# A state-space convolution and a 4-bit feed-forward layer in one kernel: kernels of the first 16 heads made in groups of six and ten

## The chip, the core and the metric

The kernel runs on one core of one Trainium2 chip. The metric is the device time of one execution in microseconds (us). The core has a matrix engine (PE, with PEld for its weight loads), a vector engine (DVE), a scalar engine (ACT), GpSimd (POOL) and a sync engine (SP) whose queue issues most DMAs. Each engine works through its own queue in order and waits for others by semaphores.

## The reference

Input `x` is [32, 64, 1024] (batch, head, time). A diagonal state-space layer makes one causal convolution kernel of length 1024 for each of 64 heads and applies it under a length mask. A gated feed-forward layer follows, with 4-bit weights, and its result is added to `x`:

```python
K = 2.0 * einsum('hn,hnl->hl', Cs, exp(dtA[:, :, None] * arange(1024))).real
y = irfft(rfft(u * mask, 2048) * rfft(K, 2048))[..., :1024] + u * mask * D
y = y * mask
Wg, Wu, Wd = dequant(gate), dequant(up), dequant(down)
out = x + (silu(y2 @ Wg) * (y2 @ Wu)) @ Wd      # rows are (batch, head), 1024 columns
```

## The kernel before, in words

**Kernels of the heads.** A convolution kernel of 1024 taps is a 32 x 32 product of two factors over the 128 complex state parts. For a group of heads, `phase_tables` (L182 to L210) makes eight DVE steps (L192 to L204) that leave reduced phases in `r1` and `r2`, then four ACT steps: sine twice (L207) and square twice (L209). `decay_tables` (L165) makes the decay factors `xd`, one small exponential per head on ACT. `kernel_factors` (L213 to L224) turns both into `e1` and `e2` by five DVE steps. `make_kernel` (L421) multiplies them on PE in f32 (one tap row for `D`, L425, then two passes a head, L427), rounds the result to an f16 high part on ACT (L430) and a low part on DVE (L431), and writes both to `kpad` in DRAM by two DMAs on ACT's queue (L433). `toeplitz` (L512) then reads each head back on SP's queue as a 512 KB Toeplitz tile (L525). SP is in order: while one load waits for `kpad`, everything behind it on SP waits.

**Convolution.** `conv_head` does 24 f16 matmuls per head (L548). After each pair of heads DVE masks the result (`y`, L560), ACT makes the high half `xh` (L563) and POOL the low half `xl` (L565; DVE for head 15). `conv_split` and `conv_load` split the input of four heads into `uh` (ACT) and `ul` (DVE), L495, L497, L507 and L510.

**The lead.** Before the first convolution come the parameters, `head_coefficients` for 32 heads (short DVE steps in three sections), the decay tables of heads 0 to 15, then tables, factors, kernel and loads of heads 0 to 3, the same for heads 4 to 7, and tables and factors of heads 8 to 15. `busy` (L889) issues f32 matmuls whose result nobody reads: 16 passes behind the first kernel, 8 behind the second. The low part of the input, `conv_split(k)`, stands behind the factors.

**Events.** The loop `for i, _ in enumerate(c.conv(0))` steps through the convolution of heads 0 to 15, eight steps a head, and starts other work at given steps: at step 7 `kernel_8` (kernel of heads 8 to 15, decay tables of heads 16 to 31, input split 2 and 3, tables and factors of heads 16 to 23), at 56 the scale ratios of the feed-forward weights (`scale_ratios`, L410 to L418), at 63 ten more `busy` calls, at 75 the kernel of heads 16 to 23, at 87 the input of heads 16 to 19. Weight unpacking (L578 to L599) and the group of heads 24 to 31 (`group_24`) step along at further places.

**Order.** The instructions are put in order on each queue before the kernel runs, by program order and dependencies with some moves to fill gaps. `with c.after(key)` ties the instructions of the block on an engine behind the instruction of that engine that `mark` stored under `key`.

**Behind the lead.** The feed-forward stages follow; the first one (`gu_one`, L664 and L665 on PE) runs interleaved with the convolution of heads 16 to 31.

Of the kernel before, what the change touches and what calls it, by code (L numbers as in the profile page):

```python
# [163 lines left out]

def decay_tables(nc, pool, co, cst, h0):  # L165
    xd = pool.tile([128, 8, 64], F32, name=f"xd{h0 // 8}", bufs=1, tag=f"xd{h0 // 8 % 4}")
    for h in range(8):
        nc.scalar.activation(xd[:, h, :], cst[:, 0:64], AF.Exp, scale=co["na"][:, h0 + h:h0 + h + 1])
    return xd

# [12 lines left out]
def phase_tables(nc, side, pool, co, cst, h0, nh):  # L183
# [19 lines left out]
    stt(r1, r1, off1, pl, ALU.subtract, ALU.subtract)  # L203
    stt(r2, r2, off2, pl[:, :, 32:], ALU.subtract, ALU.subtract)  # L204
    yield
    for r in (r1, r2):
        nc.scalar.activation(r, r, AF.Sin, scale=3.1415925)  # L207
    for r in (r1, r2):
        sq_op = nc.scalar.activation(r, r, AF.Square, scale=1.4142135623730951)  # L209
    return r1, r2, sq_op  # L210


def kernel_factors(nc, pool, co, xd, s1, s2, h0, nh):  # L213
    tt, stt = nc.vector.tensor_tensor, nc.vector.scalar_tensor_tensor
    per = lambda a: a[:, h0:h0 + nh].unsqueeze(2).to_broadcast([128, nh, 32])
    t = lambda name: pool.tile([128, 8, 32], F32, name=name, bufs=2)[:, :nh, :]
    e1, e2 = t("e1t"), t("e2t")
    stt(e2, s1[:, :, :32], 1.0, xd[:, :, :32], ALU.subtract, ALU.mult)
    stt(e1, s1[:, :, 32:], 1.0, per(co["ab"][:, 0]), ALU.subtract, ALU.mult)
    yield  # L220
    stt(s2, s2, 1.0, per(co["ab"][:, 1]), ALU.subtract, ALU.mult)
    tt(e1, e1, s2, ALU.add)
    last = tt(e1, e1, xd[:, :, 32:], ALU.mult)
    return e1, e2, last  # L224
# [34 lines left out]
class Core:  # L259
# [145 lines left out]
    def scale_ratios(self, s16, nt, g, name, last_factor):  # L405
# [3 lines left out]
        s, z = self.take([128, nt, g], F32), self.take([128, nt, g], F32)  # L409
        nc.scalar.copy(s, s16)  # L410
        for t0, t1, p0, p1, f in last_factor:
# [9 lines left out]
    def make_kernel(self, pool, h0, nh, place):  # L421
# [4 lines left out]
        for h in range(nh):  # L426
            nc.tensor.matmul(q[:, h, :], e1[:, h, :], e2[:, h, :], start=False, stop=(h == nh - 1),  # L427
                             skip_group_check=True)
        kb = pool.tile([32, 2, 8, 32], F16, name="kb", bufs=2)[:, :, :nh, :]
        self.mark("act", nc.scalar.activation(kb[:, 0], q, AF.Copy, scale=KSCALE))  # L430
        self.mark(("kb", h0), nc.vector.scalar_tensor_tensor(kb[:, 1], q, KSCALE, kb[:, 0], ALU.mult, ALU.subtract))  # L431
        for k in range(2):
# [9 lines left out]

    def tables(self, pool, h0, nh):
        held = h0 >= 24
        steps = phase_tables(self.nc, self.nc.vector, pool, self.co, self.cst, h0, nh)
        while True:
            try:
                with self.after("dve" if held else None), self.after("act" if held else None):
                    next(steps)
            except StopIteration as done:  # L450
                self.tab, sq_op = done.value[:2], done.value[2]
                break
            self.dve(800)
# [37 lines left out]

    def conv_split(self, k, after, last="e"):
        u, uh, ul = self.us[k]
        with self.after(("sq", after)):
            self.nc.scalar.copy(uh, u)  # L495
        with self.after((last, after)):
            self.nc.vector.tensor_tensor(ul, u, uh, ALU.subtract)  # L497
        self.us[k] = uh, ul

    def conv_load(self, h0):  # L500
        nc = self.nc
        u = self.cv.tile([128, 8, 4, B], F32, name="u", bufs=1)
        self.mark("sp", nc.sync.dma_start(u.rearrange("p c h b -> p (c h b)"), self.io["xF"][h0 // 4]))
        uh = self.cv.tile([128, 8, 4, B], F16, name="uh")
# [339 lines left out]
def tile_ssm_ffn(ctx, tc, io):  # L844
# [38 lines left out]
    c.taps(kg, 16)  # L883
    xd = [decay_tables(nc, kg, co, c.cst, h0) for h0 in (0, 8)]
    section(steps)
# [3 lines left out]
    def busy(h0, n):  # L889
        e1, e2 = (e.rearrange("p h n -> p (h n)") for e in c.fac[h0])  # L890
        for _ in range(n):
            nc.tensor.matmul(c.psum("wq", "b")[:, 0, :128], e1, e2, start=True, stop=True)

    for k, h0 in enumerate((0, 4)):
        every(c.tables(tables, h0, 4))
        every(c.factors(kg, h0, 4, xd[0][:, h0:h0 + 4]))
        c.make_kernel(kg, h0, 4, "b")
        for h in range(h0, h0 + 4):
            c.t0[h] = c.toeplitz(h)
        busy(h0, 8 - 4 * k)  # L900
        c.conv_split(k, h0)
    every(c.tables(kg, 8, 8))
    every(c.factors(kg, 8, 8, xd[1]))
    c.masks()
    tc.no_sync_barrier()

    def group_24():
        yield from c.tables(kg, 24, 8)
        yield from c.factors(kg, 24, 8, xd[3])
        while c.forced:  # L910
# [16 lines left out]

    def kernel_8():
        c.make_kernel(kg, 8, 8, "b")
        with c.after("act"):  # L930
            xd.extend(decay_tables(nc, kg, co, c.cst, h0) for h0 in (16, 24))
        for k in (2, 3):
            c.conv_split(k, 8, "kb")
        steps = c.tables(kg, 16, 8)
        next(steps)
        next(steps)
        with c.after(("kb", 8)):
            every(steps)
        every(c.factors(kg, 16, 8, xd[2]))

    def load_16():
        c.us[4] = c.conv_load(16)

    events = {7: kernel_8, 63: lambda: busy(4, 10), 56: ratios_gu, 87: load_16, 75: lambda: c.make_kernel(kg, 16, 8, "b")}
    for i, _ in enumerate(c.conv(0)):
        if i in events:
            with c.after("dve" if i == 56 else None):
                events[i]()
        if i in (32, 40, 48, 56, 64, 72, 104, 116, 124):
            next(unpack_it)  # L950
# [170 lines left out]
```

## Time and profile before

| quantity | value |
| --- | --- |
| time of three runs | 1069.36, 1070.72, 1071.31 us (median 1070.72) |
| profiled execution | 1069.87 us, of it span 1068.1 us |
| mean granted clock of PE | 0.996 |
| PE busy | 1023.9 us (96%) |
| DVE busy | 807.2 us (76%) |
| ACT busy | 775.7 us (73%) |
| POOL busy | 247.2 us (23%) |
| first matmul of the first convolution | 24.38 us from the span's start |
| last matmul of head 15 ends | 58.3 us |
| first feed-forward matmul (L664) | 62.00 us |

Times in the text are counted from the start of the span. A line of the timeline has the start, the length, engine, source line, operation, tiles out and in, shape and count; in brackets stands the idle time before it and what ended it. A line that merges several instructions (x24) has the length of all together. A line of the chain of waits has start, length, and what the chain ran through.

### The profile page before, as it was taken

What the parts mean: (1) busy time and instruction counts of PE and PEld (TensorE: products, weight loads), DVE (VectorE), ACT (ScalarE), POOL (GpSimd) and SP (SyncE); (2) the same over time, 40 slices, a digit from 0 to 9 for tenths busy, and PEclk for the clock granted to TensorE, in tenths of its full rate; (3) what the DMA queues carried; (4) which work ended last, traced back from release to release, by engine and by line L of the source; (5) the groups of instructions that cost most, each with busy time, mean ns of one, the idle gap of its engine ahead of it and who ended that gap; (6) DMA issues with size and microseconds to landing.
All of it is one profiled execution on the core that took longest, in us unless ns stands there. A gap on an engine that the chain in (4) does not pass through costs nothing.

```text
span 1068.1 us, 15388 instructions
## 1 busy us (share of the span) xinstructions
PE 1023.9 (96%) x5854; PEld 512.2 (48%) x5854; DVE 807.2 (76%) x938; ACT 775.7 (73%) x1036; POOL 247.2 (23%) x270
## 2 busy tenths in 40 slices
PE   3989999999899999999999999999999999999996
PEld 2867444444344445555565444444444444444442
DVE  8965788888987787886456767777787777777776
ACT  5767778787677778777777776666666667778775
POOL 0333233232332242223012112222211122102102
PEclk9999999999999999999999999999999999999999
DMA  6976311111111435448652001000000002424002
GB/s 196 331 248 205 108 70 40 40 60 40 36 54 50 140 91 164 147 135 280 214 168 99 30 30 50 20 20 18 13 21 21 20 21 62 146 79 154 34 1 79
DMA packets 52099, 99.76 MB, mean 93 GB/s; under 512 B 9524, under 2 KB 11444, under 8 KB 52024
## 3 DMA queue, kind: packets, MB, share of 16 engines
q1 hardware_dynamic: 38888, 70.09, 20.6%
q0 software_dynamic: 5280, 17.31, 4.3%
q10 hardware_dynamic: 7856, 11.37, 3.7%
q8 instruction: 46, 0.75, 0.3%
q14 instruction: 29, 0.24, 0.1%
HBM read 78.99 MB, written 19.76 MB: 92 GB/s over the span
## 4 chain that ended last, share of the span: by engine, by line
PE 78%; DVE 8%; issue 5%; ACT 5%; DMA 3%; POOL 1%; DVEq 0%; SPq 0%; ACTq 0%; POOLq 0%
PE chq L687 22%; PE chq L688 21%; PE chq L736 11%; PE chq L737 11%; PE cq L548 6%; PE chq L665 2%; PE chq L664 2%; ACT chq L640 1%; DVE chq L618 1%; DVE v L700 1%; DMA t<-kpad 1%; DVE chq L637 1%; ACT chq L620 1%; DMA xr<-xT 1%; POOL spill L310 1%
## 5 line engine op out<-in xcount | busy, mean ns | idle before, releaser
L687 PE MATMUL chq<-xh,w 128*128 128x512 f16 x1216 | 459.5, 379 | 7.7 <-DVE chq L618 3.3
L688 PE MATMUL chq<-xl,w 128*128 128x512 f16 x1216 | 457.6, 379 | 0.0
L618 DVE TENSOR_SCALAR chq<-chq,gur 128x1024 f32<-128x1024 f32 x261 | 333.3, 1290 | 93.7 <-PE chq L688 93.2
L620 ACT ACTIVATE chq<-chq,gur 128x1024 f32<-128x1024 f32 x285 | 304.4, 1085 | 86.6 <-PE chq L688 85.2
L640 ACT ACTIVATE chq<-chq,dnr 128x512 f32<-128x512 f32 x374 | 242.8, 661 | 74.1 <-PE chq L737 68.1
L736 PE MATMUL chq<-ihl,wd 128*128 128x512 f16 x672 | 253.1, 379 | 2.5 <-DVE wd L599 0.9
L737 PE MATMUL chq<-ihl,wd 128*128 128x512 f16 x672 | 252.6, 379 | 0.0
L637 DVE TENSOR_TENSOR chq<-chq,dnr 128x1024 f32<-128x1024 f32 x128 | 156.5, 1231 | 75.9 <-PE chq L737 75.2
L688 PEld LDWEIGHTS <-w 128*128 128x128 fp8e4 x1216 | 118.7, 98 | 156.2 <-issue 20.5
L687 PEld LDWEIGHTS <-w 128*128 128x128 fp8e4 x1216 | 118.8, 98 | 146.7 <-issue 1.2
L310 POOL TENSOR_TENSOR ihl<-v,ihl 128x512 f16<-128x512 f32 x42 | 48.3, 1149 | 363.5 <-ACT ihl L629 363.5
L737 PEld LDWEIGHTS <-wd 128*128 128x128 fp8e4 x672 | 65.6, 98 | 71.3 <-issue 6.7
L736 PEld LDWEIGHTS <-wd 128*128 128x128 fp8e4 x672 | 65.5, 98 | 68.4 <-DVE wd L599 2.0
L548 PEld LDWEIGHTS <-t 128*128 128x128 f16 x1152 | 80.8, 98 | 35.5 <-DMA t<-kpad 1.9
L548 PE MATMUL cq<-uh,t 128*128 128x256 f16 (+3 forms) x720 | 90.5, 226 | 1.7 <-DMA t<-kpad 1.7
L548 PE MATMUL cq<-ul,t 128*128 128x256 f16 (+3 forms) x360 | 71.5, 225 | 0.0
L565 POOL TENSOR_TENSOR xl<-y,xh 128x512 f16<-128x512 f32 x28 | 36.8, 1313 | 144.7 <-ACT xh L563 144.7
L629 ACT CAST ihl<-v 128x512 f16<-128x512 f32 x42 | 25.9, 617 | 58.8 <-DVE v L700 55.4
L700 DVE SCALAR_TENSOR_TENSOR v<-chq,gul,sg 128x1024 f32<-128x1024 f32 x38 | 48.7, 1280 | 17.2 <-PE chq L688 11.4
L310 POOL TENSOR_TENSOR spill<-v,spill 128x512 f16<-128x512 f32 x42 | 48.7, 1160 | 14.2 <-ACT spill L629 13.9
L640 ACT ACTIVATE chq<-chq,gur 128x512 f32<-128x512 f32 x66 | 43.2, 661 | 11.4 <-PE chq L665 10.2
L590 POOL TENSOR_TENSOR w<-w,z 128x256 int32<-128x256 int32 x42 | 31.6, 772 | 81.2 <-DVE w L584 77.5
(256 smaller groups left out, 826.4 us busy)
## 6 DMA issues: line engine op xcount, KB each, us to landing
t<-kpad SPq DMA_DIRECT2D x48, 512.0 KB, 4.4
spill<-spill POOLq DMA_DIRECT2D x42, 256.0 KB, 2.8
ihl<-spill ACTq DMA_DIRECT2D x42, 256.0 KB, 2.8
z<-zc SPq DMA_DIRECT2D x29, 256.0 KB, 3.6
u<-xF SPq DMA_DIRECT2D x12, 512.0 KB, 3.6
xr<-xT SPq DMA_DIRECT2D x12, 512.0 KB, 4.3
out<-xr POOLq DMA_DIRECT2D x24, 256.0 KB, 2.8
w<-qgu SPq DMA_DIRECT2D x21, 256.0 KB, 5.0
```

Of the source, the lines that this page charges most:

```text
L310: self.nc.gpsimd.tensor_tensor(out, a, b, op)
L548: nc.tensor.matmul(q[:, d:, h % 2, :], t0[:, lw, 128 * d:128 * d + 128], uu[:, 0:8 - d, h % 4, :], start=(d == 0 and k == 0 and h % 2 == 0 ...
L565: split.tensor_tensor(xl[:, :, ts], yv, xh[:, :, ts], ALU.subtract)
L618: self.mark("dve", self.nc.vector.tensor_scalar(q, q, col, None, ALU.mult))
L620: self.mark("act", self.nc.scalar.activation(q, q, AF.Copy, scale=col))
L637: self.mark("dve", self.nc.vector.tensor_tensor(q, q, cols.to_broadcast([128, 2, 512]), ALU.mult))
L640: self.mark("act", self.nc.scalar.activation(q[:, k], q[:, k], AF.Copy, scale=cols[:, k]))
L687: nc.tensor.matmul(q[:, b], lw, xh[:, g, :], start=(g == 0), stop=False, skip_group_check=True)
L688: nc.tensor.matmul(q[:, b], lw, xl[:, g, :], start=False, stop=(g == GH - 1), skip_group_check=True)
L700: nc.vector.scalar_tensor_tensor(v, q, last, self.sg.pop(ct - 21), ALU.mult, ALU.mult)
L736: nc.tensor.matmul(qs[j], lw, self.ihl[:, g, 0], start=(g == 0), stop=False, skip_group_check=True)
L737: nc.tensor.matmul(qs[j], lw, self.ihl[:, g, 1], start=False, stop=False, skip_group_check=True)
```

## The change

The lead makes kernels for six heads and then for ten. Tables for the second group stand behind the factors of the first on DVE (`("e", 0)`). The low part of input 0 stands behind the last phase step of the group of ten (`("r", 6)`), that of input 1 and the masks behind its factors. The `busy` calls behind the second small group and at step 63 are gone. Decay tables of heads 16 to 23 stand behind the kernel rounding of the group of ten, those of heads 24 to 31 behind the squares of group 16, in four pieces. Input splits 2 and 3 move behind group 16's decay tables (ACT) and phase steps (DVE). The scale ratios move from step 56 to step 80, and the input of heads 16 to 19 behind the last marked load on SP.

```diff
-def decay_tables(nc, pool, co, cst, h0):
-    xd = pool.tile([128, 8, 64], F32, name=f"xd{h0 // 8}", bufs=1, tag=f"xd{h0 // 8 % 4}")
-    for h in range(8):
-        nc.scalar.activation(xd[:, h, :], cst[:, 0:64], AF.Exp, scale=co["na"][:, h0 + h:h0 + h + 1])
-    return xd
+def decay_tables(nc, pool, co, cst, h0, nh):
+    xd = pool.tile([128, nh, 64], F32, name=f"xd{h0}")
+    for h in range(nh):
+        last = nc.scalar.activation(xd[:, h, :], cst[:, 0:64], AF.Exp, scale=co["na"][:, h0 + h:h0 + h + 1])
+    return xd, last
...
-        nc.scalar.copy(s, s16)
+        with self.after("act"):
+            nc.scalar.copy(s, s16)
...
         self.mark("act", nc.scalar.activation(kb[:, 0], q, AF.Copy, scale=KSCALE))
+        self.marks["kh", h0] = self.marks["act"]
...
-    def tables(self, pool, h0, nh):
+    def tables(self, pool, h0, nh, key=None):
...
-                with self.after("dve" if held else None), self.after("act" if held else None):
+                with self.after("dve" if held else key), self.after("act" if held else None):
                     next(steps)
...
+                self.mark(("r", h0), done.value[3])
...
-    def conv_split(self, k, after, last="e"):
+    def conv_split(self, k, act, dve):
         u, uh, ul = self.us[k]
-        with self.after(("sq", after)):
+        with self.after(act):
             self.nc.scalar.copy(uh, u)
-        with self.after((last, after)):
+        with self.after(dve):
             self.nc.vector.tensor_tensor(ul, u, uh, ALU.subtract)
...
-        self.mark("sp", nc.sync.dma_start(u.rearrange("p c h b -> p (c h b)"), self.io["xF"][h0 // 4]))
+        with self.after("sp" if h0 == 16 else None):
+            self.mark("sp", nc.sync.dma_start(u.rearrange("p c h b -> p (c h b)"), self.io["xF"][h0 // 4]))
...
-    for k, h0 in enumerate((0, 4)):
-        every(c.tables(tables, h0, 4))
-        every(c.factors(kg, h0, 4, xd[0][:, h0:h0 + 4]))
-        c.make_kernel(kg, h0, 4, "b")
-        for h in range(h0, h0 + 4):
-            c.t0[h] = c.toeplitz(h)
-        busy(h0, 8 - 4 * k)
-        c.conv_split(k, h0)
-    every(c.tables(kg, 8, 8))
-    every(c.factors(kg, 8, 8, xd[1]))
-    c.masks()
+    every(c.tables(tables, 0, 6))
+    every(c.factors(kg, 0, 6, xd[:, :6]))
+    c.make_kernel(kg, 0, 6, "b")
+    for h in range(6):
+        c.t0[h] = c.toeplitz(h)
+    busy(0, 8)
+    every(c.tables(kg, 6, 10, ("e", 0)))
+    c.conv_split(0, ("sq", 0), ("r", 6))
+    every(c.factors(kg, 6, 10, xd[:, 6:]))
+    c.conv_split(1, ("sq", 6), ("e", 6))
+    with c.after(("e", 6)):
+        c.masks()
...
-    def kernel_8():
-        c.make_kernel(kg, 8, 8, "b")
-        with c.after("act"):
-            xd.extend(decay_tables(nc, kg, co, c.cst, h0) for h0 in (16, 24))
-        for k in (2, 3):
-            c.conv_split(k, 8, "kb")
+    def late_decay(h0, key):
+        with c.after(key):
+            xd, last = decay_tables(nc, kg, co, c.cst, h0, 8)
+        c.mark(("xd", h0), last)
+        return xd
+    xd_24 = kg.tile([128, 8, 64], F32, name="xd24")
+    def decay_24(h, n):
+        for k in range(h, h + n):
+            nc.scalar.activation(xd_24[:, k], c.cst[:, 0:64], AF.Exp, scale=co["na"][:, 24 + k:25 + k])
+    def kernel_6():
+        c.make_kernel(kg, 6, 10, "b")
+        xd_16 = late_decay(16, ("kh", 6))
         steps = c.tables(kg, 16, 8)
         next(steps)
         next(steps)
-        with c.after(("kb", 8)):
+        with c.after(("kb", 6)):
             every(steps)
-        every(c.factors(kg, 16, 8, xd[2]))
+        for k in (2, 3):
+            c.conv_split(k, ("xd", 16), ("r", 16))
+        every(c.factors(kg, 16, 8, xd_16))
...
-    events = {7: kernel_8, 63: lambda: busy(4, 10), 56: ratios_gu, 87: load_16, 75: lambda: c.make_kernel(kg, 16, 8, "b")}
+    events = {7: kernel_6, 80: ratios_gu, 87: load_16, 75: lambda: c.make_kernel(kg, 16, 8, "b")}
     for i, _ in enumerate(c.conv(0)):
         if i in events:
-            with c.after("dve" if i == 56 else None):
+            with c.after("dve" if i == 80 else None):
                 events[i]()
+        if i in (70, 74, 78, 82):
+            with c.after(("sq", 16)):
+                decay_24((i - 70) // 2, 2)
```

## The prediction, made before the changed kernel ran

> **What bounds the kernel now.** The page comes first: PE is busy for 96% of the span, and only the first of its 40 slices is thin. The change lies in the first 62 us, so I read those in the timeline of PE, then SP's, then the stretches of two microseconds, then the chain of waits. PE first:
>
> ```profile
> 17.50 0.64 PE L427 MATMUL kq<-e2t,e1t 128*32 128x32 f32 x8 [13.52 <-DVE e1t L223]
> 24.38 1.69 PE L548 MATMUL cq<-ihl,w 128*128 128x256 f16 x24 [0.41 <-DMA w<-kpad]
> 28.58 0.71 PE L427 MATMUL kq<-e2t,e1t 128*32 128x32 f32 x16 [1.97 <-DVE e1t L223]
> 29.23 12.40 PE L548 MATMUL cq<-ihl,w 128*128 128x256 f16 x168
> 41.48 2.48 PE L892 MATMUL wq<-e2t,e1t 128*128 128x128 f32 x20
> 43.79 2.76 PE L548 MATMUL cq<-ihl,t 128*128 128x256 f16 x36
> 55.10 1.68 PE L548 MATMUL cq<-ihl 128*128 128x256 f16 x24 [0.72 <-DVE y L560]
> 62.00 0.38 PE L664 MATMUL chq<-xh,w 128*128 128x512 f16 x1 [0.72 <-ACT xh L563]
> ```
>
> The reader sees four delays: the factors of the first kernel at 17.5; after head 0, PE waits 1.97 us for the factors of heads 8 to 15; the filler of 2.48 us at 41.48; and 3.7 us between the end of head 15 (58.3) and the first feed-forward matmul. SP's queue:
>
> ```profile
> 20.44 11.32 SPq L525 DMA_DIRECT2D w<-kpad  x8
> 31.80 0.56 SPq L503 DMA_DIRECT2D u<-xF  x1
> 32.41 0.56 SPq L578 DMA_DIRECT2D w<-qgu  x1
> 37.11 1.39 SPq L525 DMA_DIRECT2D t<-kpad  x3
> ```
>
> Loads of heads 0 to 3 are issued from 20.44 (the first lands 3.9 us later), those of heads 4 to 7 from 29.17, of heads 8 to 15 from 37.11, each group when its `kpad` write has landed. The stretches show the clock and the transfers:
>
> ```profile
> 24.00:26.00 2.00, 1.62 (x24) 1.56 (x25) 1.97 (x5) 0.98 (x3) 0.00 (x0) 1.00 1.02 288
> 26.00:28.00 2.00, 0.61 (x6) 0.13 (x2) 1.50 (x5) 2.00 (x4) 0.00 (x0) 1.00 1.06 392
> 28.00:30.00 2.00, 1.42 (x20) 1.16 (x21) 1.70 (x4) 1.96 (x8) 0.00 (x0) 0.78 0.17 52
> 30.00:32.00 2.00, 2.00 (x19) 1.87 (x17) 1.54 (x2) 1.97 (x4) 0.00 (x0) 0.50 0.83 213
> ```
>
> (Busy time of PE, PEld, DVE, ACT, POOL, then granted clock, DMA share, GB/s.) After the gap of 1.97 us the clock falls to 0.50. The chain at the end of the first convolution:
>
> ```profile
> 58.10 0.34 issue
> 58.44 0.60 ACT xh L563
> 59.04 0.32 ACT r L209
> 59.36 2.08 ACT w L596 x2
> 61.44 0.52 ACT xh L563
> 61.98 1.05 DVE xl L565
> 63.08 0.39 PE chq L665
> ```
>
> Here ACT's queue, with an unpack in front of the last `xh`, sets the start of the feed-forward; DVE's last mask (60.04) had also stood behind a factor step of heads 24 to 31 (L221) that waited 1.35 us for ACT. From 70 to 94 us the stretches show PE busy for 12.00 of every 12.00 us, so what is gained at 62 us should reach the end.
>
> **The change, part by part.**
>
> *First kernel.* Eight phase steps of 4 heads take 2.29 us of DVE (starts 0.33 apart for L192, 0.26 for L197, and so on), of 8 heads 3.84 (0.60, 0.39): about 0.74 a group and 0.39 a head. Six heads: 3.07; ten: 4.62. Now the four-head phases run from 8.76 to 12.01, 0.96 of it coefficient steps, so six heads end at 12.8. About nine dependent coefficient steps are left. Today they are padded by the second group's phases; alone they cost 0.2 each (length of such a step) to 0.26 (distance of the first two L92): 1.8 to 2.3, so 14.6 to 15.1. ACT's sines and squares (1.1 us now, some 1.5) are done by then. The last factor steps took 1.77 for four heads with 0.68 of idle issue; I take 1.4 to 1.8. Factors at 16.0 to 16.9, middle 16.5: **1.0 earlier**. Four more PE passes at 0.08 take back 0.35. First load issued 20.44 - 0.65 = 19.8, landed 23.7. The low part of input 0, now behind the ten-head phases, ends at 16.5 + 0.3 (rounding) + 4.62 + 1.21 (L497) = 22.6, just before.
>
> *Ten heads.* Last phase step near 21; ACT took 1.5 from L203 to the first factor for eight heads, so 1.8 for ten; the low part of input 0 fills that wait. Five factor steps of 0.42 with some latency, 2.3: ready at 25.1. Head 0 ends at 23.7 + 1.7 = 25.4, so the 1.97 us wait goes. L425 (0.56, now inside that wait) and 20 passes (0.71 x 20/16 = 0.89) follow: head 1 starts at 26.9, now 29.3: **2.4 earlier**, the 0.65 of before included.
>
> *Fillers.* The filler at step 63 is 2.33 us of the chain. Was it covering a load? Input u landed 39.2, w 39.9, and head 8's 512 KB next in the queue at 390 GB/s takes 1.3: about 41.2, before head 7 ended at 41.6. So it goes whole: **2.3**. The eight passes at 22.71 lay in front of head 0's data and are worth nothing.
>
> *Is the next load there?* What is late next is head 6. The six loads are 3.1 MB; the first four took until 28.2 when issued at 20.44, so 27.6 now, and two more at 0.39 MB/us end at 30.3. The `kpad` write of ten heads is issued at 27.4 and 27.9. Such writes took 2.0 us with empty transfers (18.47 to 20.44) and 5.4 to 5.6 (23.11, 49.53) behind loads, ending some 0.8 after the load in front. I take 31.1; the bounds are 29.9 (2.0 after issue) and 33.5 (5.6 after). With 3.9 for a first load head 6 is there at 35.0 (33.8 to 37.4). PE arrives at 26.9 + 5 x 1.7 = 35.4, later if the clock is low: no stall, at worst 2.0. Behind it a load takes 1.3 to 1.9 against 1.6 to 1.7 of matmuls. Moving u behind the loads leaves SP free for them; group 16's `kpad` write and its loads move with PE.
>
> The Trainium skill (DMA: Bandwidth & Descriptors, Queues, rings and completion order) says that a DMA engine takes turns between queues by packets; a small write on ACT's queue should then not wait for all of SP's loads. The rows of 5.4 to 5.6 look rather like waiting in line; by the rule head 6 comes at the early bound, and the sum stays.
>
> *Clock.* Heads 1 to 7 took 12.34 for 168 matmuls, 73 ns each; 72 later ones took 4.7, 65 ns. The low spell costs 168 x 8 ns = 1.3. After the change PE idles from the end of the filler (about 21) to 23.7, 2.6 us, longer than the 1.97 that came before today's spell. I keep one spell: 0 gained, bounds +1.3 (none) and -1.3 (two).
>
> The Trainium skill (TensorE: Matmul & The Clock Gate, What's actually happening) speaks against dropping fillers: the gate is throttled by default, and lowers the rate to half after an idle window of about 3.4 us. By that a gap of 2.6 us might cost nothing, and the sum would be 1.3 better; the trace had a spell after 1.97 us, and I go by that.
>
> PE's sum: 2.4 + 2.3 = 4.7, so head 15 ends at 53.6 if PE stays the bound.
>
> *DVE and ACT.* From 8.76 to 60 us DVE idles only 4.5 us (unbusy time of the stretches of five). Fewer groups save 0.7 in phases and 0.3 in factors. The unpadded coefficient chain adds about 1.5 of idle, and waits of the group of 16 and roundings keep 0.3 to 1: DVE can come forward by 4.5 + 1.0 - 1.5 - 0.6 = 3.4, less than PE's 4.7. What can slip behind head 15 (heads 24 to 31) would relieve it. The ratios' 4.4 us (L413 to L418) from step 80 lie beside heads 10 to 15, under the phases of heads 24 to 31 (3.84), masks and a low part: 12 us of DVE in about 10.4 of PE. ACT gets two more table loads (1.28 each, L168 and L207): ACT is at 1.57 and 3.54 of 5 in 50 to 60, so they are covered; without that cover each is 1.28. I take DVE's 3.4, less 0.1 for rounding: **3.3 us** at the first feed-forward matmul, bounds 6.6 (PE's 4.7 plus the 1.9 that ACT and DVE lose after head 15 now) and below nothing (the third rival).
>
> **Forecast.** 1069.87 - 3.3 = 1066.6 for the profiled execution; this lies 0.85 under the median, so 1070.72 - 3.3 = 1067.4. Its own range is 1065.5 to 1069.
>
> **Rivals.**
> 1. *PE alone decides, and the end of the lead gets cleaner.* Gain 6.0 (4.7 and part of the 1.9): 1064.7. For it: the work of heads 24 to 31 need not precede the last mask. Against: DVE is full in 35 to 45 and 50 to 55 now.
> 2. *Head 6 takes the place of the wait removed.* Its load at 37.4 stalls PE 2.0, and without filler a second low spell costs 1.3: 4.7 - 3.3 = 1.4 gained, 1069.3. For it: 5.6 us writes. Against: PE is slowed before it anyway. That the order holds DVE back without an earlier first kernel (1.0 lost of DVE's 3.4) ends near here too, 1068.4.
> 3. *Slower: the last mask waits for ACT.* A factor step of heads 24 to 31 stands in front of the last mask on DVE and waits for ACT. In front of its sines ACT now also has an exponential table load (1.28), eight exponentials (2.0), the ratios' copies and scalings (1.2) and the sine table again (1.28): 5.8. If none of it finds idle ACT time, the mask is late by 5.8 against the 4.7 gained, and PE's gap, then over 5 us, costs one more low spell, 1.3: 1070.72 - 4.7 + 5.8 + 1.3 = 1073.1. It decides once more than 3.4 us of the 5.8 are uncovered. Against: the exponentials are tied only behind group 16's squares, some 10 us earlier, where ACT has room.
>
> **How the numbers follow.** Forecast 0.53, rival 1 0.13, rival 2 0.17, rival 3 0.17. A measurement here can tell 0.2%, 2.1 us, from no change: faster means under 1068.6, slower over 1072.9. The forecast's own spread leaves 0.03 of it within 0.2% and rival 2 has a small part under: faster 0.64, same 0.19, slower 0.17. The range reaches from 1064.0, below rival 1, to 1072.2, leaving out most of rival 3 and little below.
>
> **What would show it.** First factors near 16.5 and head 0 near 23.7; no gap over 0.5 before the passes of ten heads and head 1 near 27; no gap at head 6; one low-clock spell; L664 near 58.7 and everything later shifted by that. It is wrong if head 6's load lands after 38, if the last mask stands far behind head 15, or if a shift at 62 us has shrunk by 110.

## The result and the profile after

| kernel | median | runs | ratio to the kernel before, 95% interval | profiled execution, span | mean granted clock |
| --- | --- | --- | --- | --- | --- |
| before | 1070.61 us (1068.96 to 1072.1) | 20 | | 1069.87, 1068.1 us | 0.996 |
| after | 1071.86 us (1069.63 to 1073.92) | 20 | 1.0015 [1.0009, 1.0021] | 1072.38, 1070.6 us | 0.989 |

The change does not make the kernel 3.3 us faster; it is 1.25 us longer in the median and 2.5 us in the profiled execution. That is less than the 0.2% that the prediction set as its bound, but the interval leaves out 1.

The timeline of PE after the change (L552 stands for L548 of before, L428 for L427, L668 and L669 for L664 and L665):

```profile
16.41 0.85 PE L428 MATMUL kq<-e2t,e1t 128*32 128x32 f32 x12 [12.12 <-DVE e1t L223]
23.67 2.75 PE L552 MATMUL cq<-ihl,w 128*128 128x256 f16 x24 [2.80 <-DMA w<-kpad]
27.55 1.28 PE L428 MATMUL kq<-e2t,e1t 128*32 128x32 f32 x20
28.76 11.86 PE L552 MATMUL cq<-ihl,w 128*128 128x256 f16 x168
53.09 1.68 PE L552 MATMUL cq<-ihl,w 128*128 128x256 f16 x24
60.04 1.01 PE L668 MATMUL chq<-xh,w 128*128 128x512 f16 x2 [5.28 <-ACT xh L567]
61.86 0.61 PE L668 MATMUL chq<-xh,w 128*128 128x512 f16 x1 [0.80 <-ACT w L600]
62.89 0.58 PE L669 MATMUL chq<-xl,w 128*128 128x512 f16 x1 [0.42 <-DVE xl L569]
```

The front of the lead went as forecast: first factors at 16.41, head 0 at 23.67, no wait in front of the 20 passes, heads 1 to 7 in one piece. Head 15 ends at 54.77, 3.5 us earlier than before. Then PE waits 5.28 us, and the first matmul with the low half, which came at 63.08, comes at 62.89. SP's queue:

```profile
19.68 13.70 SPq L529 DMA_DIRECT2D w<-kpad  x8
33.43 1.66 SPq L529 DMA_DIRECT2D t<-kpad  x3
55.33 1.40 SPq L529 DMA_DIRECT2D t<-kpad  x3
```

The first load is issued at 19.68 (19.8 forecast). The last row holds the loads of head 16 and on. The kernel before issued them later (55.66) and still began head 16 in front of its first feed-forward matmul; the changed kernel began it only at 64.12. PE before, then after:

```profile
59.78 0.28 PE L548 MATMUL cq<-uh,t 128*128 128x256 f16 x1 [1.47 <-DMA t<-kpad]
```

```profile
64.12 0.42 PE L552 MATMUL cq<-uh,t 128*128 128x256 f16 x1
```

By 63 us the kernel before had done 27 matmuls of heads 16 and 17, the changed kernel none. The change had moved the input load of these heads from 31.80 to 49.02 on SP, and its low part (`ul`) was done at 61.70 in place of 54.45. The stretches of two microseconds, with the columns of the prediction:

```profile
24.00:26.00 2.00, 2.00 (x18) 1.86 (x16) 1.97 (x4) 0.00 (x0) 0.00 (x0) 0.51 1.03 349
28.00:30.00 2.00, 2.00 (x23) 1.64 (x22) 0.80 (x3) 1.12 (x2) 0.00 (x0) 0.50 1.03 378
58.00:60.00 2.00, 0.00 (x0) 0.00 (x0) 2.00 (x5) 1.99 (x3) 1.40 (x2) 0.54 1.01 278
60.00:62.00 2.00, 1.16 (x3) 0.24 (x3) 2.00 (x3) 1.15 (x1) 2.00 (x2) 0.50 1.05 408
66.00:68.00 2.00, 2.00 (x13) 1.16 (x11) 1.85 (x3) 0.22 (x1) 0.00 (x0) 0.50 0.72 276
```

There are two stretches at 0.50 now: 24.0 to 30.8, and 58.2 to 68.4 behind the gap. From 58 to 60 DVE and ACT are full (2.00 and 1.99 of 2.00) while PE stands still. The chain of waits names it:

```profile
52.58 1.68 DVE r L203
54.26 0.43 DVE ihl L415
54.68 0.07 DVE r L204
54.76 0.24 issue
55.00 2.32 DVE ihl L418 x4
57.33 0.07 DVE y L564
...
58.64 0.60 DVE y L564
59.24 0.80 DVE w L588
60.04 1.66 DVE ul L514
61.70 1.14 DVE xl L569
```

From 50 us to the first low-part matmul the chain holds no PE. In front of the last two masks (`y`, 57.25 and 58.57) DVE does the phase steps of heads 24 to 31 and the reciprocals of the ratios; in front of the last low half (`xl`) an unpack and the low part of heads 16 to 19.

The order in time: the mask of heads 18 and 19 starts 3.4 us later than before. DVE before, then after:

```profile
75.17 0.69 DVE L560 TENSOR_TENSOR y<-cq,mask 128x512 f32<-128x512 f32 x1 [1.31 <-PE cq L548]
```

```profile
78.54 0.69 DVE L564 TENSOR_TENSOR y<-cq,mask 128x512 f32<-128x512 f32 x1 [1.25 <-PE cq L552]
```

So 0.2 earlier at 63 us has become 3.4 later at 75 us. In between lie the rest of the stretch at half clock and the matmuls of heads 16 and 17 that the kernel before already had behind it. From there the distance is passed on (3.9 at 161 us, 2.5 at 915 us).

### The profile page after: what moved, and what is told of

Its sections match the earlier page's. It is cut to its first block, busy times and chain, and to the rows that moved or that the text cites. A ratio compares the mean times of both kernels' runs of the same rounds, so it can differ in the third digit from the quotient of the medians.

```text
span 1070.6 us, 15308 instructions
## 1 busy us (share of the span) xinstructions
PE 1023.9 (96%) x5824; PEld 509.8 (48%) x5824; DVE 807.1 (75%) x924; ACT 778.0 (73%) x1033; POOL 244.8 (23%) x270
## 4 chain that ended last, share of the span: by engine, by line
PE 78%; DVE 9%; issue 5%; ACT 5%; DMA 2%; POOL 1%; DVEq 0%; ACTq 0%; POOLq 0%; SPq 0%
PE chq L691 21%; PE chq L692 21%; PE chq L740 12%; PE chq L741 12%; PE cq L552 6%; PE chq L669 2%; PE chq L668 2%; DVE chq L622 1%; DVE v L704 1%; ACT chq L624 1%; DVE chq L641 1%; ACT chq L644 1%; ACT sg L699 1%; DMA xr<-xT 1%; PE chq L745 1%
## 5 line engine op out<-in xcount | busy, mean ns | idle before, releaser
L691 PE MATMUL chq<-xh,w 128*128 128x512 f16 x1216 | 460.0, 379 | 7.4 <-DVE chq L622 3.3
L644 ACT ACTIVATE chq<-chq,dnr 128x512 f32<-128x512 f32 x374 | 242.8, 661 | 74.6 <-PE chq L741 68.4
L552 PEld LDWEIGHTS <-t 128*128 128x128 f16 x1152 | 81.8, 98 | 35.2 <-issue 1.7
L552 PE MATMUL cq<-uh,t 128*128 128x256 f16 (+3 forms) x720 | 91.8, 228 | 0.5 <-DMA t<-kpad 0.5
L552 PE MATMUL cq<-ul,t 128*128 128x256 f16 (+3 forms) x360 | 72.4, 228 | 0.0
L569 POOL TENSOR_TENSOR xl<-y,xh 128x512 f16<-128x512 f32 x28 | 33.7, 1204 | 149.8 <-ACT xh L567 139.0
L668 PE MATMUL chq<-xh,w 128*128 128x512 f16 x128 | 49.6, 390 | 6.3 <-ACT xh L567 5.3
```

The costliest lines, as they stand in the source:

```text
L552: nc.tensor.matmul(q[:, d:, h % 2, :], t0[:, lw, 128 * d:128 * d + 128], uu[:, 0:8 - d, h % 4, :], start=(d == 0 and k == 0 and h % 2 == 0 ...
L644: self.mark("act", self.nc.scalar.activation(q[:, k], q[:, k], AF.Copy, scale=cols[:, k]))
L668: nc.tensor.matmul(q[:, k], lw, xh[:, g, :], start=(g == 0), stop=False, skip_group_check=True)
L691: nc.tensor.matmul(q[:, b], lw, xh[:, g, :], start=(g == 0), stop=False, skip_group_check=True)
```

## The experiments

Each kernel was timed in five rounds against the kernel before on the same chip. Two theories were held against each other. **Queues:** PE is no longer the bound from head 15 on; in-order queues of DVE and ACT, loaded with work of later stages, set the start of the feed-forward near 60 to 62 us whatever PE does. **Rivals:** exponential table loads on ACT, the clock, or the loads of head 16 are the cause.

| run | what differs | ratio, 95% interval | runs | mean granted clock |
| --- | --- | --- | --- | --- |
| e1 | after, ratios at 56 | 1.0011 [1.0001, 1.0021] | 12 | 0.9918 |
| e2 | after, decays of 24 to 31 early | 1.0028 [1.0017, 1.0039] | 9 | 0.9913 |
| e4 | after, tables of 24 to 31 late | 1.0020 [1.0010, 1.0031] | 12 | 0.9921 |
| e8 | e1, sines later | 1.0011 [1.0002, 1.0021] | 11 | 0.9922 |
| e10 | before, sines later | 0.9999 [0.9990, 1.0008] | 11 | 0.9959 |
| e9 | e1, late work behind the loop | 0.9993 [0.9984, 1.0002] | 11 | 0.9926 |
| e11 | e9, kernel of 16 first on ACT | 0.9999 [0.9989, 1.0009] | 11 | 0.9927 |
| e12 | e9, low half first | 0.9987 [0.9977, 0.9996] | 12 | 0.9946 |
| e18 | before, late order of e12 | 1.0008 [1.0000, 1.0017] | 11 | 0.9952 |
| e19 | e12, ratios at 80 | 1.0008 [0.9997, 1.0019] | 11 | 0.9937 |
| e5 | before, two fillers out | 1.0000 [0.9991, 1.0009] | 11 | 0.9951 |
| e3, e7, e13 | after, e1, e12 with a filler in the gap | 1.0013, 1.0015, 1.0006 | 11 each | 0.9940, 0.9939, 0.9965 |
| e16, e17 | before, after with two spill buffers | 0.9998, 1.0025 | 11, 8 | 0.9957, 0.9924 |
| e14, e15 | e12, e13 with two spill buffers | 0.9994, 1.0000 | 11 each | 0.9933, 0.9949 |

The mean clock is that over the timed runs; the kernel before had 0.9958 to 0.9965 in its own.

### e1, e8, e10: what stands in front of the last mask

e1 undoes one part of the change:

```diff
-    events = {7: kernel_6, 80: ratios_gu, 87: load_16, ...}
+    events = {7: kernel_6, 56: ratios_gu, 87: load_16, ...}
-            with c.after("dve" if i == 80 else None):
+            with c.after("dve" if i == 56 else None):
```

> The changed kernel with the scale ratios back at step 56. Theory A (DVE's queue between heads 13 and 15 sets the start of the feed-forward: reciprocals of 2.3 us and a mask at 57.25 behind them): the mask of heads 12 and 13 comes 3 us earlier, the first matmul on a low part (now 62.9) near 60, and the time is 2 to 4 us under the changed kernel's 1071.9. Rival B (ACT's late exponentials and two more table loads set it): less than 0.7 us of change, since ACT has the same work. Rival C (the transfers of the third weight unit and of u set it): no change.

Measured: 1071.02 us against 1069.44. The mask of heads 12 and 13 comes 2.6 us earlier (54.64), the last one hardly, and the ratio (1.0011) is that of the change within the intervals, not the 2 to 4 us less that theory A expected. DVE's timeline of e1:

```profile
57.13 1.35 DVE L221 SCALAR_TENSOR_TENSOR r<-r,ab 128x256 f32<-128x256 f32 x1 [1.83 <-ACT r L209]
58.41 0.68 DVE L564 TENSOR_TENSOR y<-cq,mask 128x512 f32<-128x512 f32 x1
```

With the reciprocals gone from there, a factor step of heads 24 to 31 waits 1.83 us for ACT in front of the last mask: the prediction's third rival, here with a smaller price. The ratios are one link of the queue, not the whole of it. e8 moves that link too, by putting the last step of the group of 24 (sines and squares) at step 126, and e10 does so in the kernel before:

```diff
-        if i in (80, 86, 92, 98, 104, 110):
+        if i in (80, 86, 92, 98, 104, 126):
```

> The changed kernel with the ratios at step 56 and the sines and squares of heads 24 to 31 at step 126 in place of 110; the factor step that stood in front of the last mask in the run with the ratios at 56 now stands behind the last low half. Theory A, now in this form: what sets the start of the feed-forward is DVE's and ACT's queues in front of the last mask, high half and low half, not PE. Then the last mask comes within 1 us of the end of head 15 (55.0), the first matmul on a low part at 57.5 to 59.5 (62.9 in the changed kernel), PE's gap shrinks from 5.3 to under 3.5, and the time is 2.5 to 5 us under the changed kernel, 1.5 to 4 under the one before. If the third weight unit's unpacking sets it instead: the masks come early but the first feed-forward matmuls stay at 61 or later and the time is within 1 us of the run with the ratios alone.

> The kernel before with nothing changed but the sines and squares of heads 24 to 31 at step 126 in place of 110. On DVE the factor step that waited 1.35 us for ACT moves from in front of the last mask to behind the last low half. Theory A: the last mask 1.4 to 2 us earlier than 60.04, the first matmul on a low part at 61 to 62 (63.08), the time 0.5 to 2 us under the kernel before. If PE sets the start: no change.

Measured: in e8 both masks are early (54.57 and 55.69), and the time is that of e1. ACT's timeline of e8:

```profile
56.38 2.19 ACT L600 ACTIVATE w<-w,cst 128x1024 fp8e4<-128x1024 uint8 x2 [0.48 <-POOL w L594]
58.47 1.03 ACT L511 CAST uh<-u 128x1024 f16<-128x1024 f32 x1
59.40 0.61 ACT L567 CAST xh<-y 128x512 f16<-128x512 f32 x1
```

The last high half (`xh`) stands behind two unpacks and the high part of heads 16 to 19, and ends at 60.0 though its mask was done at 56.4. The wait went from DVE to ACT. In e10's profile the last mask comes at 57.52 in place of 60.04 and the first low-part matmul 0.8 us earlier (62.32), and the median does not change (1070.44 against 1070.32); why not is not shown.

### e2, e4: the group of heads 24 to 31

e2 puts its exponentials behind those of heads 16 to 23, which saves two table loads on ACT; e4 puts its table steps later.

```diff
+        with c.after(("kh", 6)):
+            decay_24(0, 8)
...
-        if i in (70, 74, 78, 82):
-            with c.after(("sq", 16)):
-                decay_24((i - 70) // 2, 2)
```

```diff
-        if i in (80, 86, 92, 98, 104, 110):
+        if i in (112, 114, 116, 118, 120, 122):
```

> The changed kernel with the decay tables of heads 24 to 31 right behind those of heads 16 to 23, so two ACT table loads fewer. Rival B: the first matmul on a low part comes 2 us or more earlier than 62.9 and the time falls by 2 to 4 us. Theory A: the reciprocals still stand in front of the masks, less than 1 us of change.

> The changed kernel with the tables of heads 24 to 31 started at step 112 in place of 80, so that most of their 4 us of DVE stand behind the masks. Theory A: the first matmul on a low part 2 to 4 us earlier than 62.9, time 2 to 5 us lower. Rival B: ACT loses the second sine load in front of the last high half too, 1.3 us earlier at most. Rival C: no change.

Measured: both are slower than the kernel before, e2 with 1072.51 us and e4 with 1071.49. In the timelines of PE the gap grows, to 6.67 in e2 and 7.30 in e4. In e4 the last mask is done by 59.34, but ACT waits 2.90 us for POOL in front of an unpack at 59.35, with `uh` and `xh` queued behind it, and `xh` starts at 61.34: a later place inside the loop only puts other work in front. In e2 the two table loads are gone and the time is no better, so they alone are not the price; there, too, ACT waits 3.04 us for POOL in front of an unpack (58.31), with `uh` and `xh` queued behind it.

### e9, e12, e11: the late work out of the way

e9 is e1 with the last two table steps of heads 24 to 31, the third weight unit's unpack and the halves of heads 16 to 19 written behind the loop. e12 adds that these table steps stand behind the last low half on DVE. e11 is e9 with a higher priority for the kernel of heads 16 to 23.

```diff
-        if i in (32, 40, 48, 56, 64, 72, 104, 116, 124):
+        if i in (32, 40, 48, 56, 64, 72, 104):
             next(unpack_it)
-        if i in (80, 86, 92, 98, 104, 110):
+        if i in (80, 86, 92, 98):
             next(group_it)
+    next(unpack_it)
+    next(unpack_it)
+    c.us[4] = c.conv_load(16, c.u16)
+    with c.after("low"):        # e12; without it in e9
+        next(group_it)
+        next(group_it)
```

> The changed kernel with the ratios back at step 56, the last two table steps of heads 24 to 31 behind the loop, and the unpack of the third weight unit and the halves of heads 16 to 19 written behind the last high half, so that no work of a later stage stands on ACT or DVE in front of the last two masks and their halves. Theory (the in-order queues of ACT and DVE set the start of the feed-forward): last mask near 55.5, last high half on ACT at 56 to 57, low half of DVE at 57 to 58.5, first feed-forward matmul near 57, PE idle for under 3 us behind head 15 and no stretch at a clock of 0.50 there; the time is 2 to 4 us under the changed kernel and at least 1 us under the kernel before (1067 to 1069). Rival (the kpad loads of head 16, which land near 60, or the third weight unit set the pace): the first matmul may come at 57, but PE then waits 2 to 4 us a little later, the work at 75 us is no earlier than 77.5, and the time is within 1 us of the changed kernel.

> The run with the late work of ACT and DVE behind the loop (last table steps, third unit's unpack, halves of heads 16 to 19), with one more order: the last two table steps (L203, L204 of heads 24 to 31, 2.2 us there) stand behind the last low half on DVE. Theory (in-order queues): the low half follows the last high half at once, near 57.5 to 58 in place of 58.84, the first low-part matmul near 58.3 in place of 59.57, the second wait of 1.45 us goes; the time is 1 to 1.5 us under that run, and 3 us more if no stretch at a clock of 0.50 follows: 1065.5 to 1069. Rival (the weight units on POOL and the kpad loads of head 16 set what follows 58 us): PE waits there instead, the work near 76 us is no earlier, the time is within 0.7 us of that run.

> The run before, and the kernel of heads 16 to 23 (matmuls, rounding, kpad write) placed by the scheduler with a higher priority, so that ACT rounds it ahead of the exponentials and of the third unit's unpack. Theory: its write is issued at 46 to 47 rather than 49 to 50 and the loads of head 16 near 51 to 52; its matmuls can then fill what PE would idle behind head 15, the gap shrinks to under 1.5 us, and the time is a further 0.5 to 2 us under the run before. Rival (the write lands with the loads that stand in front of it and not by its own issue): the loads of head 16 still land near 60, and the time is that of the run before within 0.5 us.

Measured: e9 1069.64 us, e12 1068.53, e11 1070.70. The timelines of PE and DVE in e12:

```profile
54.67 1.68 PE L555 MATMUL cq<-ihl,w 128*128 128x256 f16 x24
57.86 0.59 PE L673 MATMUL chq<-xh,w 128*128 128x512 f16 x2 [1.51 <-ACT xh L570]
59.29 0.61 PE L674 MATMUL chq<-xl,w 128*128 128x512 f16 x1 [0.85 <-DVE xl L572]
```

```profile
56.46 0.69 DVE L567 TENSOR_TENSOR y<-cq,mask 128x512 f32<-128x512 f32 x1 [0.86 <-PE cq L555]
57.07 0.61 DVE L593 TENSOR_SCALAR w<-w,cst 128x1024 uint16<-128x1024 uint16 x1
57.84 1.40 DVE L572 TENSOR_TENSOR xl<-y,xh 128x512 f16<-128x512 f32 x1 [0.16 <-ACT xh L570]
```

Now the last mask waits for PE, as it should, and the gap of PE is 1.51 us in place of 5.28. The low-part matmul comes at 59.29, 3.6 earlier than in the changed kernel. Taken by the ratios, e12 is 1.0015 - 0.9987 = 0.28% or 3.0 us under the changed kernel and 0.13% or 1.4 us under the kernel before: the only run whose interval against the kernel before lies under 1. e9 differs from it by less than the intervals tell, and e14 below, which is e12 with one more buffer, got 0.9994, so the 1.4 us may be too much; among eighteen experiments, one such interval is weak evidence of a gain in time. What the traces do show is the start near 59 us. In e11 the `kpad` write is issued at 47.24 but the loads of head 16 still at 55.61, behind the input load and weight loads on SP (53.93 to 55.5); what the rival expected came, by SP's order.

### e18, e19: the change's own gain, or that of the order

e18 gives the kernel before the same late order; e19 is e12 with the ratios left where the change puts them.

> The kernel before with the same order of its late work as in the run with the low half first (last two table steps behind the last low half, third unit's unpack and halves of heads 16 to 19 behind the loop), the groups of four, four and eight kept. Theory (the change takes 3 to 4 us off PE's share of the lead, and the late order lets it through): here the late order alone can only take what ACT and DVE lose behind head 15, 62.0 becomes 60.3 at best, head 15 still ends near 58: ratio to before 0.9988 to 1.0000, and above that of the next run by 0.001 or more. Rival (the late order alone is what was gained, the groups of six and ten bring nothing): ratio 0.998 to 0.9990, as with the change.

> The changed kernel, its ratios left at step 80, with the late order (last two table steps behind the last low half, third unit's unpack and halves of heads 16 to 19 behind the loop). Theory (queues): the reciprocals of the ratios (2.3 us of DVE) lie in front of the last two masks again but 2 to 3 us of later work no longer do; last mask near 57, last low half near 58.5, start of the feed-forward 57.5 to 59; ratio 0.9985 to 1.0000, 0.0005 to 0.001 above the run with the ratios at 56. Rival (the ratios' place is what cost the change its gain): the last mask at 59 or later, ratio 1.0010 or more.

Measured: both 1.0008. The first feed-forward matmul in PE's timelines of e18 and e19:

```profile
58.60 0.59 PE L669 MATMUL chq<-xh,w 128*128 128x512 f16 x2 [1.51 <-ACT xh L566]
```

```profile
58.60 1.01 PE L673 MATMUL chq<-xh,w 128*128 128x512 f16 x2 [3.81 <-ACT xh L570]
```

The late order alone gains nothing on the kernel before: the interval of e18 (from 1.0000) does not meet that of e12 (to 0.9996). So what e12 gains, if it holds, needs the lead of the change: its groups, the fillers left out and the new places of decay tables and input splits, which no run takes apart. In e19 head 15 ends at 54.80, but four reciprocals (2.34 us) stand in front of the last two masks, and PE waits 3.81. The ratios' place costs the gap 2.3 us; its interval (from 0.9997) just leaves out that of e12. This fell between the two expectations: the masks came when the theory said, the ratio near the rival's.

### e5, e3, e7, e13: fillers and the clock

e5 takes the filler at step 63 and the one behind the second group out of the kernel before. e3, e7 and e13 put matmuls without use behind head 15, into the changed kernel (14 calls), e1 (14) and e12 (8).

```diff
-    events = {7: kernel_8, 63: lambda: busy(4, 10), 56: ratios_gu, ...}
+    events = {7: kernel_8, 56: ratios_gu, ...}
```

```diff
+    e1, e2 = (e[:, :4].rearrange("p h n -> p (h n)") for e in c.fac[16])
+    for _ in range(14):
+        nc.tensor.matmul(c.psum("wq", "a")[:, 0, :128], e1, e2, start=True, stop=True)
```

> The kernel before without the filler at step 63 and behind the second group. By the prediction's term the whole 2.3 us should arrive at the end. Theory A: the end of head 15 comes up to 2.3 us earlier, the first matmul on a low part stays at 63.1 within 0.7, the gap widens by the same and the time is the same or, with a low-clock spell in the gap, up to 3 us longer.

> The changed kernel with 14 matmuls whose result nobody reads (28 passes, about 3.5 us) behind head 15, in the 5.3 us in which PE now idles. If the low clock costs what the stretches suggest (0.50 from 58 to 68 us, PE busy in some 5.5 us of it): the first matmul on a low part stays at 62.9, the clock stays at 1.00, and the time falls by 2.5 to 3 us. If the later loss has another cause: the same time as the changed kernel within 0.7 us.

> The changed kernel with the ratios at step 56 and the filler of 28 passes behind head 15. The queue in front of the last mask still waits 1.8 us for ACT, so the first matmul on a low part stays near 61.5; the clock stays at 1.00 through the gap, which saves about 1.5 us against the run with the ratios alone (its low spell was 57.8 to 64.6). If the clock is worth nothing: the same time as that run.

> The same, with 8 matmuls without use directly behind head 15 (2 us at full clock, into a bank that no mask waits for). Theory of the clock: what remains of the gap behind head 15 is then covered and no stretch at 0.50 follows between 56 and 66 us in the profile, the matmuls up to 66 us cost 3 us less in a profile that would have had it, and the time is 0.5 to 2 us under the run without them. Rival (the low clock of the lead is decided by the phase of its own interval and not by this gap): the stretch comes as often as without, and the time is the same within 0.7 us or up to 0.7 us longer, as the matmuls without use push the first feed-forward matmul back.

Measured: e5 has the time of before (1069.91 against 1070.32). Head 15 ends 1.1 us earlier, not 2.3; two waits took the filler's place. PE's timeline of e5:

```profile
40.89 1.69 PE L548 MATMUL cq<-ihl,t 128*128 128x256 f16 x24 [1.31 <-DVE ihl L414]
43.34 1.24 PE L548 MATMUL cq<-ihl,t 128*128 128x256 f16 x12 [0.76 <-DMA t<-kpad]
```

The fillers in the gap do lift the clock: by 0.0028, 0.0021 and 0.0019 of the span, which is 3.0, 2.2 and 2.0 us. But none of the three kernels is faster than its partner by more than the intervals tell, and e13 is slower (1.0006 against 0.9987). e7's filler itself waited 1.66 us for a mask and pushed the start to 63.60. So the clock given back did not show as time. For the first spell e3's profile shows why. It has no stretch at 0.50 at all, and head 15 ends at 54.83, as in the changed kernel (54.77): without the slow spell PE waits for the load of head 6 instead. PE's timeline of e3:

```profile
26.75 7.80 PE L552 MATMUL cq<-ihl,w 128*128 128x256 f16 x120
36.78 1.69 PE L552 MATMUL cq<-ihl,w 128*128 128x256 f16 x24 [2.23 <-DMA w<-kpad]
```

For the second spell it shows a price: the mask of heads 18 and 19 is at 75.29, 3.2 earlier than in the changed kernel, and this execution took 1069.43 us. But it is the fastest of e3's eleven, whose median is 1070.56.

### e14 to e17: does a gain at 73 us reach the end?

In e13 the mask of heads 18 and 19 came at 72.9, 2.3 ahead of the kernel before; the lead was 1.9 at 137 us and gone at 161. ACT's timeline of e13 shows a wait there:

```profile
141.95 0.62 ACT L638 CAST spill<-v 128x512 f16<-128x512 f32 x1 [2.20 <-DMA spill<-spill]
146.52 0.62 ACT L638 CAST spill<-v 128x512 f16<-128x512 f32 x1 [1.69 <-DMA spill<-spill]
```

The products of the second batch half have one buffer, whose store (2.3 to 4.6 us to landing) the next cast waits for; before, these waits were 0 and 0.59. Four kernels got a second buffer.

```diff
-            hl = self.fw.tile([128, 2, 512], F16, name="spill", bufs=1)
+            hl = self.fw.tile([128, 2, 512], F16, name="spill", bufs=2)
```

> The run with late work behind the loop and the low half first, with two spill buffers. Theory S: ACT's wait of 2.25 us on the spill store at 147.65 goes, PE is busy 9.3 or more of 10.00 in 140 to 150 in place of 8.11, and the time is 1 to 2 us under the run with one buffer: ratio to before 0.997 to 0.998. Rival: PE's idle time of 140 to 150 has another cause (the rescalings of chq on ACT and DVE), it comes back within 20 us and the ratio stays at 0.9987 within 0.0007.

> The same with the 8 matmuls without use behind head 15, and two spill buffers. Theory S: the waits of 2.20 and 1.69 us at 142 and 146.5 go, PE is busy 9.3 or more of 10.00 in 140 to 150 in place of 7.51, the 2.3 us that this kernel is ahead of the kernel before at 73 us are still there at 161 us, and the time is 2 to 3 us under before: ratio 0.9972 to 0.9985 in place of 1.0006. Rival: the ratio stays within 0.0007 of 1.0006, and what was ahead at 73 us is lost in another stage behind 160 us.

> The kernel before with two spill buffers. Theory S: its wait at 146 us is 0.59, at 168.6 0.66, so at most 1.2 us can go: 1069.4 to 1070.5. Rival: the time of before within 0.4 us.

> The changed kernel with two buffers in place of one for the spill of the second batch half (the buffer that the cast of the next product, on ACT, waits for until the store has landed). Theory S (the spill store eats what the lead gains): the changed kernel gains nothing in its lead at 75 us, so there is little for the store to eat; its own waits there are 0.83 us at 150 us and some 1 us of PE: 0 to 1.2 us under the changed kernel, 1070.5 to 1072 by the earlier runs. Rival (the store is no bound of PE at all): the changed kernel's time within 0.5 us.

Measured: 1068.94, 1069.82, 1069.64 and 1072.17 us; before 1069.39. In e14 the waits on the store are gone and in e15 one of 1.82 is left; PE is busy 8.93 (e14) and 9.45 (e15) of 10.00 in 140 to 150 us, in place of 8.11 and 7.51. But the ratios do not follow: e14 and e12 overlap, and so do e15 and e13. In the profiled e15 the work at 915 us is 1.3 ahead of the kernel before, and its median is not. The store's wait is real and its removal shows in its place, but it is not shown to be what takes the gain; that stays open.

## Why the prediction was wrong

**The first kernel, the ten heads: right.** Factors 16.41 (16.5 forecast), first load 19.68 (19.8), head 0 at 23.67 (23.7). The wait of 1.97 us is gone.

**Heads 1 to 7: "no stall, at worst 2.0" fell.** Head 1 was to start at 26.9 and started at 28.76: "I keep one spell" held for the number, but it lasts 6.8 us and begins under head 0, whose 24 matmuls took 2.75 in place of 1.69, and the 20 passes 1.28 in place of the 0.89 forecast. Yet the clock is not what took the 1.2 us that are missing at head 15 (3.5 gained of the 4.7). Without the spell (e3) head 1 starts at 26.75, as forecast, and PE then waits 2.23 us for head 6, whose load was issued at 32.83 (31.1 forecast) and let PE go on at 36.78 (35.0). With a spell of 3.4 us (e1, e13) it waits 0.47 and 0.35 there, and head 15 ends at 54.99 and 55.04. So rival 2's late load is there; in the changed kernel's profile the spell of 6.8 us hides it.

**The filler: "So it goes whole: 2.3" fell.** Alone it is worth 1.1 at head 15 and nothing in time (e5): it lay over waits for DVE and for a load.

**DVE and ACT: the step that failed.** "DVE can come forward by 4.5 + 1.0 - 1.5 - 0.6 = 3.4" and "I take DVE's 3.4 ... at the first feed-forward matmul". The first low-part matmul came forward by 0.19, the first matmul by 1.96. The sum took DVE's idle time (4.5) as free but for the coefficient chain's 1.5 and 0.6 of waits. The waits of DVE between 22 and 60 us in the changed kernel (who waited for what: us in total, times, the longest):

```profile
DVE e2t L218 <- ACT r L209: 2.4, 2, 2.2
DVE y L564 <- PE cq L552: 1.4, 2, 1.0
DVE kb L433 <- ACT kb L431: 1.2, 1, 1.2
DVE ihl L414 <- ACT ihl L411: 0.5, 1, 0.5
```

That is 5.5 us, where the kernel before has 4.4 in the same view. The longest, 2.21 us at 37.84, is for ACT, which makes the exponentials of heads 16 to 23, loads the sine table (1.28 at 34.54) and only then the squares. Before, DVE did the low parts of inputs 2 and 3 (30.74 and 32.94) and the first ratio steps (39.29 and 40.93) in front of that point; the change moves both behind it, and nothing is left to fill the wait. With the ratios alone put back (e1) it is 2.68; the low parts put back were not tried. And the sum never asked in which order DVE would do its work: "What can slip behind head 15 (heads 24 to 31) would relieve it" is possible (e12 does it, and gets 3.6 us at the low-part matmul), but the order written in the change does not: the last mask started at 58.57, 3.8 us behind head 15, which the prediction had named as a sign of being wrong. Phase steps, reciprocals, unpack and `ul` stood in front of the last masks and the last low half.

**The gap's price: left out of the forecast, named in rival 3.** "PE's gap, then over 5 us, costs one more low spell, 1.3". The gap came (5.28), and the stretch at 0.50 was 10.2 us long. Up to 62.89 PE waits in it, for an unpack and the low half, so only the 5.5 us of work from 62.89 to 68.4 count: 2.8 lost, as an estimate. The 27 matmuls of heads 16 and 17 are a second term, which the prediction did not have: 24 take 1.53 us at full clock (55.10 to 56.63 before), so 27 take 1.7; two more feed-forward matmuls done by then (0.22 each) take 0.4 off. Together that is 4.1, where 3.6 were lost between 63 and 75 us. e3, at full clock, lost 1.6 there (first low-part matmul 61.60, 1.5 ahead of before; mask 75.29, 0.1 behind), so about 2.0 are left for the clock.

The mean clock of the 20 runs, 0.9912 against 0.9959 in the runs of before beside e1 to e4, is lower by 0.0047, or 5.0 of 1069 us; the median is longer by 1.25. That fits the traces, in which much of the low clock lies where PE waits anyway: over head 6's load, and in the gap.

**"What is gained at 62 us should reach the end"** was not tested by the change, which gained nothing there. Where a run did gain (e13), it was lost by 161 us.

**Rival 3** was nearest in sign and in its place, the last masks. Its queue was another: not the exponentials' table loads (e2) but reciprocals, phase steps, unpack and `uh`, one behind the other (e1, e8, e12). The measured distance is +1.25 in place of +2.4.

What makes up the 1.25 us of the median stays open. The account above is that of one execution, and the clock does not sort the others: of the 20 runs of the changed kernel, the ten with a clock of 0.992 or more have a median of 1071.75 us, the ten below it 1071.91.

## What to carry to other kernels

When the bound engine is given back time, list, for each other engine, what stands in its queue in front of the instruction that the next stage waits for; a sum of work saved says nothing about that order. Take the head of the chain away and look at the next: here reciprocals, then a factor step, then an unpack each held the same start near 60 us, and only moving all of them brought the start forward. An engine's idle time may be where the work that is about to be moved has its free place.

## What the runs showed of the hardware

**Clock stretches have a unit.** The stretches at 0.50 in the lead were 3.4, 6.8 or 10.2 us long in all profiles that had one, and came behind gaps of PE of 2.80 us (head 0, after) and 1.97 us (before). The Trainium skill (TensorE: Matmul & The Clock Gate, What's actually happening) states a free-running window of about 3.4 us and half the rate behind an idle window. The unit agrees with the trace, and the two stretches of the changed kernel begin ten units apart (24.03 and 58.16). The gaps of 1.97 and 2.80, shorter than a window and followed by 3.4 and 6.8 us at half, do not fit a rule that asks for a whole idle window, and the measurement decides.

**DVE beside POOL.** `r` (L203, 128x512) took 0.73 us in the kernel before and 1.68 after, where POOL's `xl` (1.16 us) had begun 0.03 us ahead of it. POOL's timeline and DVE's, after:

```profile
52.55 1.16 POOL L569 TENSOR_TENSOR xl<-y,xh 128x512 f16<-128x512 f32 x1 [2.71 <-ACT xh L567]
```

```profile
52.58 1.68 DVE L203 SCALAR_TENSOR_TENSOR r<-r,cst,pl 128x512 f32<-128x512 f32 x1
```

The extra 0.95 is most of POOL's 1.16. The Trainium skill (SBUF — State Buffer, SBUF: two separate sides) says that a DVE instruction with two inputs in SBUF and a GpSimd one shut each other out of a shared port for a whole instruction; the rows agree. In the kernel before they met the other way round: POOL's `xl`, begun at 55.78 while DVE went through L201 to L204 (55.58 to 57.4), took 2.68 us. The prediction's price of these phase steps (3.84 for eight heads) has no such term.
